# Letting every late place of two step lists take side steps that need exp and log

## The chip, the cores and the metric

The kernel runs on one core of a Trainium2 chip. The metric is the device time of one execution in microseconds (us), the median of several runs; lower is better. TensorE (PE in the profile, with its weight loads as PEld), VectorE (DVE), ScalarE (ACT), GpSimd (POOL) and SyncE (SP) each work through their own list of instructions in order. They wait for each other by semaphores.

## The reference

Two layers of a sequence model, each a mixer and a feed-forward part with a residual around both, on 4 sequences of 256 tokens with 512 features (1024 tokens in all):

1. retention: projections q, k, v, gate; rotary embedding; decay-weighted attention in chunks of 128; RMS norm; output projection.
2. a router: softmax over 64 logits, the 8 largest weights w of each token, `out = flat * w_sum + w_dense @ expert_bias`.
3. a state-space mixer with 128 heads in 8 groups: `proj = x @ in_proj_w.T`, a causal convolution of 4 taps and silu on most of it, per-head steps `dt = softplus(...)`, decays `exp` of cumulated `dt * A`, the chunked product, a gate `silu(gate)`, a group norm and an output projection.
4. low-rank adapters: 64 adapters of rank 16, the 16 best of each token.

In front of each part stands `_layernorm(x)`, and each adds to x. All arithmetic is float32; the large projections are three matmuls each of a high and a low part.

## The kernel before

The tokens are worked on in two halves of 512. Each stage is a pipeline over units that is written out by hand: a list of letters says in which order one turn of the loop emits its pieces of work. A scheduler then orders the instructions of each engine, within what the data and the rotation of buffers in program order allow. Bank "x" of PSUM has two buffers: whatever is allocated there in program order waits until the tile two before it has been read. The same goes for the tags "xn" (one buffer) and "xd" (two).

Stage 3 (the mixer of part 3) has 64 units: a pair of two 128-channel chunks for one half. The order is four pairs of half 0, the same four of half 1, then the halves in turn. A turn `i` works on three pairs: `before` (output projection, O0 to O3, L858), the pair itself (T0, T1: transposes and scaling, L779 to L790; M0, M1: the mixer's matmuls `ps_y`, L804) and `after` (I0, I1: x projections `ps_x`, convolution L714 and L716 and silu; G0, G1: gate projections `ps_g` and silu; X0, X1: sums of the exponents, L294 and L296; D0, D1: their exp, L1122, and the product with C.B, L757; B: `ps_bc`). W casts one weight tile into its high (ACT, L139) and low part (POOL, L142) and starts later loads.

Beside the units runs the **side line**: a queue of generators for work of other parts. In stage 3 its first entries are `route(1)` (the router for half 1: logits L603, softmax L616 to L622, top 8 L627 to L630, transposed weights L634 and L636, update of x L645 to L650) and `prepare3(1)` (half 1 for part 3: load of wdt L690, moments L87 to L92, normalised x L100 to L126, then the softplus steps L217 to L246, and the cumulated sums ps_cum, ps_in, ps_tail L250 to L268). A place P or E in a list calls `pump` (L1133), which runs one step of the queue, up to its next `yield`. A step that has to follow a use of exp or log is announced by `yield True`:

```
def pump(steps=1, table=False):
    while k.side and steps and (table or not k.needs):
        k.needs = next(k.side[0], k)
```

P is `k.pump` and does nothing while the next step needs exp or log; E is `k.pump(1, True)` and takes any step. The reason for two letters is ScalarE's tables: silu sits in one set, exp and log in another, and `act` (L1115 to L1124) puts a table load (L1119) between them and holds all uses of a set together. In a turn the silus come up to G1 and the exps at D0, D1. The side line's PSUM tiles go to bank "x" in stage 3 (`k.bank = BANK3`). Its softmax weights `wT` take a buffer of tag "xd", as `xd` of T0, T1 does; `raw_wdt`, the normalised `xn`, `room` of the softplus and `xe` of T0, T1 all take the one buffer of "xn".

Which list a turn uses is chosen at L926: FILL3 for turn -1, SIDE3 while the queue is not empty, else STEP3. Before the first pair of half 1 is prepared (turn 3), whatever is left in the queue is run off at once (L910, `k.pump(1000, True)`). At the end of the stage the router of part 4 joins the queue, and turns 63 and 64 use SIDE3 again.

Of the kernel before, what the change touches and what calls it, by code (L numbers as in the profile page):

```python
# [18 lines left out]
P = 128  # L19
# [13 lines left out]
STEP1 = "K S0 W T S1 S2 W G0 G1 K C K P U A0 K W P A1 T P P Q0 N0 W W N1 Q1 T T W K D F".split()  # L33
SIDE1 = "S0 W G0 T P K C W W P P W S1 K G1 S2 U P A0 N0 A1 P Q0 T W T F W N1 K Q1 T T D W W".split()
STEP3 = "W T0 T1 B I0 W M0 M1 X0 X1 I1 O0 G0 W W O1 W W P O2 W W G1 P W O3 D0 D1 W W".split()
FILL3 = "B X0 X1 I0 I1 P P G0 G1 W W P P W D0 D1 E E".split()
SIDE3 = "T0 T1 I0 I1 M0 M1 P B X0 X1 P P O0 W O1 G0 G1 W W P O2 O3 W P W P D0 D1 E E".split()

# [615 lines left out]
def state_space(k, tc, io):  # L656
# [239 lines left out]
    def run(done):  # L896


        with tc.tile_pool(name="s3", bufs=1, reuse_waits="tile") as own.only:
            for i in range(-1, len(pairs) + 1):  # L900
# [24 lines left out]
                )  # L925
                for one in FILL3 if i < 0 else SIDE3 if k.side else STEP3:  # L926
                    who = {"T": p, "M": p, "O": before, "P": k, "E": k, "W": k}.get(one[0], after)
# [329 lines left out]
```

## Time and profile before

| | |
|---|---|
| median of 3 runs | 2560.72 us (2560.52 to 2563.05) |
| the profiled execution's own time | 2561.88 us |
| its span, first to last instruction | 2560.1 us |
| mean granted TensorE clock | 0.988 |
| busy: PE, DVE, ACT, POOL | 2459.5, 2070.7, 1534.0, 1539.5 us |
| table loads on ACT | 193, 1283 ns each |
| stage 3 in the span | about 935 to 2440 us |
| its turns with route(1) and prepare3(1) | up to about 1057 us |

Times in the views are microseconds from the span's start. A row of the timeline is: start, duration, engine, line, operation, output<-inputs, shape, and in brackets how long the engine was idle before it and who ended that. A row of waits is: who waited, for whom, sum in us, times, longest. A row of the table by stretches is: stretch, length, then for each engine its busy time and instructions, the granted TensorE clock, the DMA share and rate.

### The profile page before, as it was taken

The numbers are of one execution on the slowest core, as the hardware profiler recorded it, in microseconds if no ns is written. First come the engines' busy times: TensorE is split into PE (matmuls) and PEld (weight loads), VectorE is DVE, ScalarE is ACT, GpSimd is POOL, SyncE is SP. The second block draws the span as 40 slices with busy tenths as digits, with TensorE's granted clock in tenths as the row PEclk, the third lists the DMA queues.
The fourth block names the chain that finished last, engine by engine and source line by source line (L and its number), as shares of the span: only waits on it lengthen the run. The fifth ranks groups of instructions, "written<-read, shape, count | busy, mean of one in ns | idle before, by whom it ended". The sixth has DMA issues, their size and how long they took to land.

```text
span 2560.1 us, 35586 instructions
## 1 busy us (share of the span) xinstructions
PE 2459.5 (96%) x13488; PEld 1991.8 (78%) x13488; DVE 2070.7 (81%) x2694; ACT 1534.0 (60%) x2109; POOL 1539.5 (60%) x996
## 2 busy tenths in 40 slices
PE   7899999999999898899999999999999999999889
PEld 6778787788777686678888888888888888888677
DVE  6787777778788779697988888988988988979963
ACT  3665565566665565475765756666756657657630
POOL 4554444546565547586784865856756756757840
PEclk9999999999999999999999999999999999999989
DMA  3222112212222222242332323222323223313321
GB/s 107 76 71 53 50 50 58 66 58 89 84 92 60 72 91 87 78 124 71 95 91 67 101 73 91 91 72 86 99 66 99 83 67 103 95 61 105 99 70 68
DMA packets 82891, 206.18 MB, mean 81 GB/s; under 512 B 8672, under 2 KB 10592, under 8 KB 82720
## 3 DMA queue, kind: packets, MB, share of 16 engines
q1 hardware_dynamic: 82720, 203.90, 26.6%
q8 instruction: 107, 1.75, 0.3%
q14 instruction: 64, 0.52, 0.1%
HBM read 200.86 MB, written 3.01 MB: 80 GB/s over the span
## 4 chain that ended last, share of the span: by engine, by line
PE 73%; DVE 17%; ACT 3%; POOL 3%; issue 3%; DMA 1%; SPq 0%; POOLq 0%; ACTq 0%; DVEq 0%
PE ps_g L201 16%; PE ps_x L201 11%; PE ps_o L858 10%; PE ps_o L459 6%; PE ps_q L201 6%; PE ps_y L804 5%; PE ps_y L412 3%; PE ps_bc L201 3%; DVE m L757 3%; DVE conv L716 3%; PE ps_sc L400 2%; PE ps_o L1084 2%; PE ps_v L201 2%; PE ps_t L779 2%; DVE m L294 2%
## 5 line engine op out<-in xcount | busy, mean ns | idle before, releaser
L201 PE MATMUL ps_g<-xs_hi,wg_h 128*128 128x512 f32 x768 | 308.8, 402 | 13.7 <-DVE r_q L354 7.3
L201 PE MATMUL ps_g<-xs_lo,wg_h 128*128 128x512 f32 x768 | 304.8, 397 | 0.0
L201 PE MATMUL ps_g<-xs_hi,wg_l 128*128 128x512 f32 x768 | 302.5, 396 | 0.0
L757 DVE TENSOR_TENSOR m<-m,cb 128x1536 f32<-128x1536 f32 x128 | 275.0, 2152 | 30.4 <-ACT m L1122 29.9
L716 DVE SCALAR_TENSOR_TENSOR conv<-ps_x,cw,conv 128x510 f32<-128x510 f32 (+2 forms) x384 | 269.9, 736 | 24.7 <-ACT conv L714 22.2
L1119 ACT ACT_TABLE_LOAD x193 | 247.6, 1283 | 3.9 <-PEq L1245 0.8
L294 POOL TENSOR_TENSOR m<-gb,start 128x512 f32<-128x512 f32 x128 | 152.8, 1196 | 128.5 <-PE ps_y L804 90.2
L142 POOL TENSOR_TENSOR wo_l<-raw_wo,wo_h 128x1024 fp32r<-128x1024 f32 x60 | 152.2, 2537 | 124.1 <-ACT wo_h L139 118.2
L858 PE MATMUL ps_o<-wo_h,yh 128*128 128x512 f32 x512 | 212.8, 416 | 13.0 <-DVE acc L864 11.1
L296 POOL TENSOR_SCALAR_AFFINE_SELECT m<-m 128x1024 f32<-128x1024 f32 x160 | 217.2, 1358 | 1.5 <-DVE m L294 1.4
L832 POOL TENSOR_TENSOR sqs<-sqs,sq 128x512 f32<-128x512 f32 x112 | 186.8, 1668 | 46.5 <-ACT sq L830 46.5
L818 POOL TENSOR_TENSOR xs<-xs,sg 128x512 f32<-128x512 f32 x128 | 204.5, 1597 | 13.8 <-DVE xs L814 13.8
L142 POOL TENSOR_TENSOR wx_l<-raw_wx,wx_h 128x1024 fp32r<-128x1024 f32 x38 | 97.8, 2575 | 178.8 <-ACT wx_h L139 168.5
L201 PE MATMUL ps_x<-xs_lo,wx_h 128*128 128x512 f32 x512 | 205.3, 401 | 0.0
L201 PE MATMUL ps_x<-xs_hi,wx_h 128*128 128x512 f32 x512 | 204.3, 399 | 0.0
L201 PE MATMUL ps_x<-xs_hi,wx_l 128*128 128x512 f32 x512 | 203.9, 398 | 0.0
L858 PE MATMUL ps_o<-wo_l,yh 128*128 128x512 f32 x512 | 203.1, 397 | 0.0
L858 PE MATMUL ps_o<-wo_h,yl 128*128 128x512 f32 x512 | 199.1, 402 | 2.5 <-DVE yl L823 2.5
L142 POOL TENSOR_TENSOR wg_l<-raw_wg,wg_h 128x1024 fp32r<-128x1024 f32 x60 | 152.7, 2545 | 63.9 <-ACT wg_h L139 63.9
L201 PEld LDWEIGHTS ps_g<-xs_hi,wg_h 128*128 128x128 f32 x768 | 144.5, 188 | 56.9 <-issue 17.3
L1122 ACT ACTIVATE xs<-conv,cb 128x512 f32<-128x512 f32 x128 | 90.8, 722 | 162.8 <-DVE conv L716 162.6
L1122 ACT ACTIVATE m<-m 128x1024 f32<-128x1024 f32 (+1 forms) x160 | 181.4, 1134 | 9.7 <-POOL m L296 9.4
(281 smaller groups left out, 6929.3 us busy)
## 6 DMA issues: line engine op xcount, KB each, us to landing
gb<-cum SPq DMA_DIRECT2D x160, 512.0 KB
raw_wx<-in_L_attn_in_x_dram SPq DMA_DIRECT2D x38, 512.0 KB
raw_wg<-in_L_attn_in_gate_dram SPq DMA_DIRECT2D x38, 512.0 KB
raw_wo<-n_L_attn_out_proj_w_dram SPq DMA_DIRECT2D x38, 512.0 KB
raw_wq<-in_L_attn_Wq_dram SPq DMA_DIRECT2D x22, 512.0 KB
raw_wg<-in_L_attn_Wg_dram SPq DMA_DIRECT2D x22, 512.0 KB
raw_wo<-in_L_attn_Wo_dram SPq DMA_DIRECT2D x22, 512.0 KB
raw_wkv<-in_L_kv_dram SPq DMA_DIRECT2D x11, 512.0 KB
```

Of the source, the lines that this page charges most:

```text
L142: nc.gpsimd.tensor_tensor(lo, w, hi.bitcast(F32), ALU.subtract)
L201: tc.nc.tensor.matmul(ps, a[:, c, :], b[:, c, :], start=(c == 0 and n == 0), stop=(c == KC - 1 and n == 2))
L294: engine.tensor_tensor(m[:, blk], gb[:, min(blk, 1)], last(at, P), ALU.add)
L296: nc.gpsimd.affine_select(out=causal, in_=causal, compare_op=ALU.is_ge, fill=GONE, base=0, pattern=[[0, 8], [1, P]], channel_multiplier=-1,)
L459: nc.tensor.matmul(ps, y[:, 2 * h + b, :], w[:, h, :], start=(i == 0), stop=(i == 5))
L716: nc.vector.scalar_tensor_tensor(acc[:, :, j:], ps[:, :, :SEQ - j], cw[:, ch, TAPS - 1 - j:TAPS - j], acc[:, :, j:], ALU.mult, ALU.add,)
L757: made = nc.vector.tensor_tensor(mh, mh, cbs[p.g, p.half].rearrange("p z b l -> p z (b l)").unsqueeze(2) .to_broadcast([P, 3, 2, 2 * P]), ...
L818: nc.gpsimd.tensor_tensor(xs, xs, p.sg[n], ALU.mult)
L832: nc.gpsimd.tensor_tensor(total, total, sq, ALU.add)
L858: nc.tensor.matmul(ps, y[:, at], w[:, n, :], start=(i == 0), stop=(i == 5))
L1119: load = nc.scalar.preload_act_table_set(table)
L1122: ins = nc.scalar.activation(out, in_, func, bias=bias, scale=scale)
```

## The change

In FILL3 the third pair of P becomes E, and in SIDE3 the three P behind G0 and G1 become E. Nothing else is touched.

```
-FILL3 = "B X0 X1 I0 I1 P P G0 G1 W W P P W D0 D1 E E".split()
-SIDE3 = "T0 T1 I0 I1 M0 M1 P B X0 X1 P P O0 W O1 G0 G1 W W P O2 O3 W P W P D0 D1 E E".split()
+FILL3 = "B X0 X1 I0 I1 P P G0 G1 W W E E W D0 D1 E E".split()
+SIDE3 = "T0 T1 I0 I1 M0 M1 P B X0 X1 P P O0 W O1 G0 G1 W W E O2 O3 W E W E D0 D1 E E".split()
```

Counted through the generators, the queue's steps fall on the turns of stage 3 as follows:

| turn | before | changed |
|---|---|---|
| -1 | moments and logits of the router | the same |
| 0 | max and exp; sum and top 8 | the same two, then wT, update of x tiles 4, 5 |
| 1 | wT, x tiles 4 to 7, load of wdt, moments, first normalised tile | x tiles 6, 7, load of wdt, moments, all four normalised tiles |
| 2 | normalised tiles 5 to 7, dt projection, softplus up to log | dt projection, softplus, ps_cum, ps_in, ps_tail |
| 3, run off at once | ps_cum, ps_in, ps_tail | nothing |
| 63, 64 | router of part 4 | the same steps at the same places |

## The prediction

> **What bounds the kernel now.** I read the busy times and the chain first, then the table by stretches, the waits and the timeline around the only place the step table of the change touches, turns 0 to 3 of stage 3.
>
> ```profile
> PE 2459.5 (96%) x13488; PEld 1991.8 (78%) x13488; DVE 2070.7 (81%) x2694; ACT 1534.0 (60%) x2109; POOL 1539.5 (60%) x996
> ...
> PE 73%; DVE 17%; ACT 3%; POOL 3%; issue 3%; DMA 1%; SPq 0%; POOLq 0%; ACTq 0%; DVEq 0%
> ```
>
> TensorE bounds the whole. Turns 0 to 3 are among the few places where it doesn't. The table by stretches (stretch, length, busy PE, PEld, DVE, ACT, POOL, clock, DMA share, GB/s):
>
> ```profile
> 963.80:980.00 16.20, 16.20 (x142) 13.99 (x142) 16.20 (x22) 9.54 (x14) 15.21 (x9) 1.00 0.44 135
> 980.00:1004.00 24.00, 20.41 (x76) 13.14 (x75) 22.64 (x39) 17.88 (x26) 17.22 (x21) 0.93 0.28 96
> 1004.00:1011.30 7.30, 4.79 (x14) 3.37 (x14) 7.15 (x12) 0.00 (x0) 2.79 (x4) 0.77 0.22 72
> 1011.30:1030.00 18.70, 15.21 (x104) 11.61 (x103) 15.19 (x23) 10.54 (x16) 12.69 (x12) 0.91 0.09 30
> 1030.00:1045.50 15.50, 13.73 (x58) 10.05 (x58) 12.33 (x14) 5.22 (x8) 7.12 (x4) 1.00 0.11 34
> 1045.50:1052.50 7.00, 0.05 (x2) 0.03 (x1) 6.79 (x6) 1.55 (x2) 3.86 (x2) 0.74 0.47 150
> ```
>
> From 980 to 1052.5, PE is idle for 3.6 + 2.5 + 3.5 + 1.8 + 7.0 = 18.4 us, and DVE is nearly full where PE is emptiest: the side line paces this part. The longest single wait, from the waits view and the timeline:
>
> ```profile
> PE ps_cum L250 <- DVE e L246: 6.9, 1, 6.9
> ...
> POOL rstd L91 <- DVE mv L89: 6.6, 3, 4.0
> ```
> ```profile
> 1043.00 0.69 DVE L237 SCALAR_TENSOR_TENSOR e<-room,e 128x512 f32<-128x512 f32 x1
> 1044.72 2.44 DVE L238 SCALAR_TENSOR_TENSOR start<-room,start 128x512 f32<-128x512 f32 x1 [1.02 <-ACT start L1122]
> 1047.19 2.72 DVE L240 SCALAR_TENSOR_TENSOR dt<-dt,start 128x512 f32<-128x512 f32 x1
> 1049.83 0.68 DVE L241 TENSOR_TENSOR e<-e,room 128x512 f32<-128x512 f32 x1
> ```
>
> The softplus chain runs on DVE alone while PE stands still. L238 and L240 take 2.44 and 2.72 us where L237, of the same shape, takes 0.69: POOL is splitting wo and wx (L142, 2.4 us each) just then. That surplus I call lock time.
>
> **What the change removes, adds and moves.** No instruction is added: the built program has 193 table loads as before, and the same work on each engine. Turn -1 and turns 63, 64 take the same steps; there only neighbours swap at the very end of the program (6 matmuls of 0.23 us, one store behind one load), for which I allow 1 us either way and take 0. All else is order within about 965 to 1057 us. Three edits decide.
>
> (1) In turn 3 nothing is left to run off; ps_cum follows turn 2's work. (2) The four normalised tiles move into turn 1, in front of turn 2's x projections. (3) wT and the first two updates of x move into turn 0, in front of turn 1's. Edits 2 and 3 have a price: bank "x" rotates in program order through two buffers, so `ps_x` of pair 2 must now wait until `x += ps_o_4` is done, and `ps_x` of pair 3 behind the four transposed tiles. wT also takes the "xd" buffer that the xd of pair 1 needs, so pair 1's `ps_y` waits for the last router matmul. The built order shows it: `ps_x` of pair 2 stands behind ps_o_4 and ps_o_5, `ps_y` of pair 1 behind ps_o_7. On POOL the exponents of pair 2 (L294), which were at 978.6, now stand behind the four pairs of rstd instructions (L91, L92), which wait for DVE's moments. Queued behind them: the gating (L818) that ACT's yh and so `ps_o` wait for, and the splits of wdt and wbc.
>
> I lay the rows of the timeline end to end in the new order, between four marks: end of `ps_y` of pair 0 (966.8), of pair 1 (979.55), of pair 2 (1022.0), start of ps_cum (1052.5). Before: 12.7 + 42.5 + 30.5 = 85.7 us.
>
> First stretch. The logits of tile 7 come some 3 us earlier, at about 973. DVE then: L607 0.2, L616 0.4, L617 0.35, L757 1.75, L620 to L622 1.0, L627 and L628 1.3, L630 and L629 0.7 (to about 980); POOL's nine small ones 2.15, some of it behind L630; four L645 2.9 (to 984.4). PE meanwhile has 24 `ps_o` and 24 `ps_g` (5.6 us each at a start-to-start of 0.233), wT comes at 985, ps_o_4 ends at 987, and its add (0.67) frees the bank at 987.7. Then 24 `ps_x` 5.6 (993.3), ACT L714 0.7, three L716 and an L650 (996.9), ps_o_7 1.1, xd 0.68, xe 0.41, 24 `ps_y` 2.6: about 1001.8. That is 35.0 us: **+22.3**.
>
> Second stretch. POOL sets it: rstd out at about 1001.5, then L294 1.2, L818 1.65, L296 1.3, again 1.2 and 1.65, L832 1.3, L296 1.3, wdt 1.3, wbc 2.35 = 13.3 us (1015); the load of wo takes the buffer that wbc frees, 3.6 us from issue to cast (997.81 to 1001.40), and its cast (1.05) stands in front of xs_hi on ACT; then 0.59 + 0.69 + 0.65 for the tile (1021.6), 48 matmuls of `ps_x` and `ps_y` in their new order 8.4: 1030. That is 28.2 us: **-14.3**.
>
> Third stretch. dt 2.8, then DVE in order: L217 0.74, xd 0.68, L823 0.75, L222 0.69, L232 0.69, xd 0.68 with a wait of 0.6, L757 1.75, L823 0.75, L234 0.43, L237 0.69, L757 1.75, L238 2.44, L240 2.72, L241, L242, L246 0.69 each, L244 0.43, and four L864 of 0.67 that now stand between them = 23.3, say 23.5: **-7.0**. The 6.95 us stall thus shrinks rather than goes: the 18 `ps_o` that now fill PE there bring their L864 into the chain.
>
> Sum **+1.0**. The rows I used for the first two stretches are free of lock time. Before has about 10 us of it between 966 and 1040 (each DVE row less the shortest of its form, summed). How much of it the new order puts on the path no row shows: none gives +1.0, all gives +11. I take a quarter, 2.5, since most lock time there fell where DVE then waited anyway. The lower bound also takes L238 and L240 free (-3.8) and half of wo's landing hidden (-1.8): -4.6. So **+3.5 us**.
>
> The clock: matmuls at 1008.28 start 0.43 us apart instead of 0.23 after a gap of no more than 2.51 us.
>
> ```profile
> 1006.88 0.50 PE L858 MATMUL ps_o<-wo_h,yh 128*128 128x512 f32 x1 [2.51 <-DVE acc L864]
> ...
> 1007.91 0.58 PE L858 MATMUL ps_o<-wo_l,yh 128*128 128x512 f32 x1
> 1008.28 0.63 PE L858 MATMUL ps_o<-wo_h,yl 128*128 128x512 f32 x1
> ```
>
> So many short gaps cost clock as one long gap does (0.64 from 1052.5 to 1057), and I take no gain from dividing the stall. The Trainium skill (TensorE: Matmul & The Clock Gate, "What's actually happening") has the clock halve only after an idle window of about 3.4 us; by it the divided stall would keep the full clock in those 4.5 us, and my estimate from that page would be 1.6 us lower.
>
> Against the profiled execution (2561.88 us, of which 2560.1 is span) +3.5 gives 2565.4; the median of the runs shown lies 1.2 lower, so **2564.2**.
>
> **Rivals.**
> *Faster.* The moved steps find cover: PE's waits of 6.95 (ps_cum) and 2.51 (L864) go, and edits 2 and 3 add only what PE lacks in the first stretch. It has there 17.3 us of work (24 `ps_o`, 24 `ps_g`, two ps_o of the router, transposes, logits) for the 20.7 us until the bank is free: 3.4. Sum -9.5 + 3.4 = -6.1: 2554.6. For it: PE is what fills most of the chain. Against it: DVE is busy 94% from 980 to 1004 and cannot take the router's chain sooner for nothing.
>
> *Slower.* The bank makes pair 2's projections late, POOL's row behind the rstds makes everything of pair 2 late, and all the lock time falls on that path, because POOL's and DVE's queues are now both on it: +11, 2571.7. It decides from a quarter of the 10 us upwards: +5.1 is reached at 4.1 us of lock time. For it: L757 was hit for 1.8 and L823 for 1.0 in a stretch where POOL split wbc, and these now stand side by side with the same split. Against it: the third stretch is shorter by rows that already hold their lock time.
>
> *Nothing changes.* The places take the same steps: true of turns -1, 63, 64, false of turns 0 to 3 by the count of steps; so it gets no chance of its own.
>
> **Numbers.** What a measurement of this kernel can tell from no change is about 0.2%, 5.1 us. Forecast case (-2.8 to +5.1): 0.50. Faster: 0.17, of which 0.12 lies beyond 0.2%. Slower: 0.33, all beyond. So faster 0.12, same 0.55, slower 0.33. The range takes in the lower bound of -4.6 and, above, the slow rival: 2555.5 to 2572.
>
> **What would show it.** Right: PE's wait for L246 at ps_cum falls below about 4 us, `ps_x` of pair 2 starts near 988 instead of 967, `ps_y` of pair 1 ends near 1002, L294 of pair 2 on POOL stands behind L92, and ps_cum starts between 1050 and 1058. Wrong: ps_cum before 1048 (then the lock time and POOL's row were overpriced), or after 1060; a difference made anywhere behind 1060, where both programs have the same order until the last 120 us, would mean that my whole frame misses.

## The result, and the profile after

The changed kernel takes **2576.32 us** (median of 4 runs, 2574.43 to 2579.27); the kernel before took 2561.89 us beside it (4 runs, 2560.52 to 2565.36). The ratio is **1.0049, interval 1.0036 to 1.0061**: slower by 14.4 us by the medians and by 12.6 by the ratio, where +3.5 was forecast. The time lies outside the range given. The profiled execution took 2574.43 us, 2572.7 of it span, at a mean clock of 0.987.

The lines of the page that answer to those shown of before (busy time by engine, then the chain):

```profile
PE 2465.6 (96%) x13488; PEld 1994.2 (78%) x13488; DVE 2076.9 (81%) x2694; ACT 1535.5 (60%) x2109; POOL 1542.9 (60%) x996
...
PE 72%; DVE 16%; ACT 4%; POOL 4%; issue 3%; DMA 1%; SPq 0%; POOLq 0%; ACTq 0%; DVEq 0%
```

As many instructions on each engine as before, and PE busy for 6.1 us more with them. The marks of the prediction (ends of `ps_y` of pairs 0, 1, 2, start of ps_cum) now stand at 965.7, 1002.7, 1038.7 and 1068.4. The table by stretches between these marks, first of the changed kernel, then of the kernel before (stretch, length, busy PE, PEld, DVE, ACT, POOL, clock, DMA share, GB/s):

```profile
965.70:1002.70 37.00, 31.68 (x163) 23.86 (x164) 29.83 (x55) 16.86 (x24) 16.01 (x24) 0.91 0.17 57
1002.70:1038.70 36.00, 23.90 (x121) 16.91 (x121) 25.29 (x27) 15.52 (x21) 20.20 (x13) 0.81 0.22 66
1038.70:1068.40 29.70, 20.82 (x73) 14.72 (x73) 27.82 (x27) 12.15 (x16) 23.03 (x11) 0.83 0.22 71
```
```profile
966.80:979.60 12.80, 12.80 (x107) 10.99 (x107) 12.80 (x18) 8.12 (x11) 11.81 (x7) 1.00 0.38 124
979.60:1022.00 42.40, 35.28 (x169) 24.69 (x169) 37.52 (x63) 21.87 (x32) 25.25 (x30) 0.92 0.23 70
1022.00:1052.50 30.50, 19.31 (x82) 13.86 (x81) 26.98 (x30) 13.32 (x18) 18.82 (x10) 0.89 0.20 68
```

The sum went from 85.7 to 102.7 us, **+17.0**. Subtract PE's busy time from the length: PE stood idle for 26.3 us instead of 18.3 (+8.0) and was busy for 76.4 instead of 67.4 (+9.0), with 354 records between the marks in both. The clock column goes with the second part: length times (1 - clock), summed over the stretches, is 6.8 us before and 15.2 after. So in PE's account about half of the loss is waiting, and the other half is the same matmuls at a lower clock. This says where PE's time went, not yet why: the two can trade places, as in h1_hold below, which loses 1.8 us less to the clock than before and waits 1.3 us more, in the same sum.

In the first stretch two rows come some 21 and 25 us later, both behind the router. `ps_x` of pair 2 starts at 988.30, and the second `xd` of pair 1 (L781) stands right behind the last router matmuls (L649). The changed kernel, then before:

```profile
988.30 0.50 PE L201 MATMUL ps_x<-xs_hi,wx_h 128*128 128x512 f32 x1
...
997.16 1.13 PE L649 MATMUL ps_o<-room,wT 64*128 64x512 f32 x2 [1.42 <-DVE x L650]
...
998.32 0.69 DVE L781 TENSOR_TENSOR xd<-ps_t,dt 128x512 f32<-128x512 f32 x1
```
```profile
967.15 0.48 PE L201 MATMUL ps_x<-xs_hi,wx_h 128*128 128x512 f32 x1
...
973.55 0.68 DVE L781 TENSOR_TENSOR xd<-ps_t,dt 128x512 f32<-128x512 f32 x1
```

Behind turn 3 the two programs run alike: pairs 4, 30 and 62 end 15.5, 15.4 and 15.7 us later than before (`ps_cum` starts 15.9 later, and not 17.0, because the first mark is 1.1 earlier). Some 3 us come back behind that, so that the span is 12.6 longer.

PE's timeline of the changed kernel in the second and third stretch (start, duration, what, and in brackets the idle time before it and who ended it), with the longer waits and three rows without one:

```profile
1005.38 0.50 PE L858 MATMUL ps_o<-wo_h,yh 128*128 128x512 f32 x1 [1.13 <-ACT yh L822]
...
1011.15 0.50 PE L858 MATMUL ps_o<-wo_h,yh 128*128 128x512 f32 x1 [3.75 <-ACT yh L822]
...
1019.65 0.66 PE L108 MATMUL ps_xn<-ident,xn 128*128 128x128 f32 x4 [2.10 <-DVE xn L100]
1021.30 0.65 PE L108 MATMUL ps_xn<-ident,xn 128*128 128x128 f32 x4 [1.00 <-DVE xn L100]
1024.63 1.12 PE L108 MATMUL ps_xn<-ident,xn 128*128 128x128 f32 x4 [2.67 <-DVE xn L100]
1026.38 1.11 PE L108 MATMUL ps_xn<-ident,xn 128*128 128x128 f32 x4 [0.64 <-DVE xn L100]
1027.23 0.77 PE L201 MATMUL ps_x<-xs_hi,wx_h 128*128 128x512 f32 x1
1027.80 0.63 PE L201 MATMUL ps_x<-xs_lo,wx_h 128*128 128x512 f32 x1
1028.22 0.63 PE L201 MATMUL ps_x<-xs_hi,wx_l 128*128 128x512 f32 x1
...
1049.57 0.80 PE L201 MATMUL ps_g<-xs_hi,wg_l 128*128 128x512 f32 x1 [2.73 <-POOL wg_l L142]
...
1060.83 0.80 PE L858 MATMUL ps_o<-wo_h,yh 128*128 128x512 f32 x1 [3.53 <-DVE acc L864]
...
1068.38 1.16 PE L250 MATMUL ps_cum<-upper,e 128*128 128x128 f32 x8 [1.84 <-DVE e L246]
```

The four normalised tiles come one by one, PE waits for each of them for 0.6 to 2.7 us, and then the `ps_x` of pair 3 start 0.43 us apart where 0.23 is the pace at full clock: the short waits are paid a second time in the clock. At the end of the third stretch the waits view has

```profile
PE ps_cum L250 <- DVE e L246: 1.8, 1, 1.8
```

where before had 6.9. The stall that the change aims at is gone, and the stretch is only 0.8 us shorter. The softplus rows on DVE, and the rows of POOL beside them:

```profile
1048.33 2.80 DVE L757 TENSOR_TENSOR m<-m,cb 128x1536 f32<-128x1536 f32 x1 [0.44 <-ACT m L1122]
...
1054.09 1.68 DVE L237 SCALAR_TENSOR_TENSOR e<-room,e 128x512 f32<-128x512 f32 x1
...
1057.35 2.82 DVE L238 SCALAR_TENSOR_TENSOR start<-room,start 128x512 f32<-128x512 f32 x1
...
1060.69 2.26 DVE L240 SCALAR_TENSOR_TENSOR dt<-dt,start 128x512 f32<-128x512 f32 x1
```
```profile
1037.45 1.04 POOL L294 TENSOR_TENSOR m<-gb,start 128x512 f32<-128x512 f32 x1 [13.16 <-PE ps_y L804]
1038.45 2.86 POOL L142 TENSOR_TENSOR wx_l<-raw_wx,wx_h 128x1024 fp32r<-128x1024 f32 x1
...
1055.88 3.74 POOL L142 TENSOR_TENSOR wo_l<-raw_wo,wo_h 128x1024 fp32r<-128x1024 f32 x1 [0.67 <-ACT wo_h L139]
1059.59 2.81 POOL L142 TENSOR_TENSOR wx_l<-raw_wx,wx_h 128x1024 fp32r<-128x1024 f32 x1
```

POOL's L294 of pair 3 waits 13.16 us for pair 2's `ps_y`. Of the splits behind it, three (`wg_l` at 1046.70 and the last two rows) run beside the softplus, of which L237, L238 and L240 take 1.7 to 2.8 us. DVE is idle for only 29.70 - 27.82 = 1.88 us of this stretch, so the length of its rows paces it.

### The profile page after: what moved, and what is told of

It is laid out like the page before. It is cut to its first block, busy times and chain, and to the rows that moved or that the text cites. A ratio compares the mean times of both kernels' runs of the same rounds, so it can differ in the third digit from the quotient of the medians.

```text
span 2572.7 us, 35585 instructions
## 1 busy us (share of the span) xinstructions
PE 2465.6 (96%) x13488; PEld 1994.2 (78%) x13488; DVE 2076.9 (81%) x2694; ACT 1535.5 (60%) x2109; POOL 1542.9 (60%) x996
## 3 DMA queue, kind: packets, MB, share of 16 engines
q8 instruction: 107, 1.75, 0.3%
## 4 chain that ended last, share of the span: by engine, by line
PE 72%; DVE 16%; POOL 4%; ACT 4%; issue 3%; DMA 1%; SPq 0%; POOLq 0%; ACTq 0%; DVEq 0%
PE ps_g L201 15%; PE ps_x L201 11%; PE ps_o L858 10%; PE ps_o L459 6%; PE ps_q L201 6%; PE ps_y L804 5%; PE ps_y L412 3%; PE ps_bc L201 3%; PE ps_sc L400 2%; DVE conv L716 2%; DVE m L757 2%; PE ps_v L201 2%; PE ps_o L1084 2%; PE ps_t L779 2%; DVE m L294 1%
## 5 line engine op out<-in xcount | busy, mean ns | idle before, releaser
L201 PE MATMUL ps_g<-xs_hi,wg_h 128*128 128x512 f32 x768 | 308.9, 402 | 15.4 <-DVE r_q L354 7.1
L757 DVE TENSOR_TENSOR m<-m,cb 128x1536 f32<-128x1536 f32 x128 | 277.4, 2171 | 30.9 <-ACT m L1122 30.6
L294 POOL TENSOR_TENSOR m<-gb,start 128x512 f32<-128x512 f32 x128 | 153.7, 1203 | 142.1 <-PE ps_y L804 103.5
L858 PE MATMUL ps_o<-wo_h,yh 128*128 128x512 f32 x512 | 213.9, 418 | 17.1 <-DVE acc L864 12.2
L832 POOL TENSOR_TENSOR sqs<-sqs,sq 128x512 f32<-128x512 f32 x112 | 187.1, 1671 | 45.8 <-ACT sq L830 45.8
L818 POOL TENSOR_TENSOR xs<-xs,sg 128x512 f32<-128x512 f32 x128 | 205.5, 1606 | 12.5 <-DVE xs L814 12.5
```

Source lines behind the costliest of these rows:

```text
L201: tc.nc.tensor.matmul(ps, a[:, c, :], b[:, c, :], start=(c == 0 and n == 0), stop=(c == KC - 1 and n == 2))
L294: engine.tensor_tensor(m[:, blk], gb[:, min(blk, 1)], last(at, P), ALU.add)
L757: made = nc.vector.tensor_tensor(mh, mh, cbs[p.g, p.half].rearrange("p z b l -> p z (b l)").unsqueeze(2) .to_broadcast([P, 3, 2, 2 * P]), ...
L818: nc.gpsimd.tensor_tensor(xs, xs, p.sg[n], ALU.mult)
L832: nc.gpsimd.tensor_tensor(total, total, sq, ALU.add)
L858: nc.tensor.matmul(ps, y[:, at], w[:, n, :], start=(i == 0), stop=(i == 5))
```

## The experiments

Ratios are to the kernel before on the same chip, with the 95% interval. The three stretches are those between the four marks, in one profiled execution of each kernel; "idle" is PE's idle time in them, "clock" the length lost to a granted clock below 1 in them (summed from the profile's clock records, which is why before and after read 6.9 and 15.4 here).

| run | stretches | sum | idle | clock | ratio |
|---|---|---|---|---|---|
| before | 12.8, 42.4, 30.5 | 85.7 | 18.3 | 6.9 | 1 |
| changed | 37.0, 36.0, 29.7 | 102.7 | 26.3 | 15.4 | 1.0049 [1.0036, 1.0061] |
| h1_hold | 12.8, 42.5, 30.4 | 85.7 | 19.6 | 5.1 | 1.0002 [0.9992, 1.0011] |
| d1_one | 38.6, 32.1, 28.9 | 99.6 | 25.6 | 13.9 | 1.0056 [1.0039, 1.0074] |
| d2_two | 37.0, 33.5, 28.6 | 99.1 | 24.3 | 11.9 | 1.0043 [1.0029, 1.0058] |
| x1_wt | 15.4, 47.3, 29.1 | 91.8 | 22.3 | 8.5 | 1.0047 [1.0032, 1.0062] |
| t3_bank_after | 35.1, 32.4, 28.7 | 96.2 | 27.8 | 17.1 | 1.0091 [1.0074, 1.0108] |
| t4_bank_before | 11.9, 44.5, 39.0 | 95.4 | 24.7 | 14.8 | 1.0089 [1.0074, 1.0104] |
| t5_bank_wt | 12.0, 50.9, 28.6 | 91.5 | 21.0 | 13.2 | 1.0066 [1.0051, 1.0081] |
| t7_local | 12.0, 51.0, 28.5 | 91.5 | 20.9 | 13.1 | 1.0028 [1.0016, 1.0041] |
| n1_wdt | 39.7, 29.4, 30.4 | 99.5 | 25.6 | 13.7 | 1.0063 [1.0047, 1.0079] |
| k1_no_split | 39.7, 32.6, 22.3 | 94.6 | 23.9 | 11.1 | 1.0042 [1.0027, 1.0057] |
| k2_before_no_split | 12.7, 37.5, 27.1 | 77.3 | 12.7 | 3.7 | 0.9969 [0.9959, 0.9980] |
| b1_before_wt | 12.8, 40.1, 30.4 | 83.3 | 17.2 | 5.8 | 0.9983 [0.9973, 0.9992] |
| b1_again | 12.8, 38.4, 30.5 | 81.7 | 17.3 | 4.1 | 0.9985 [0.9975, 0.9995] |
| g1_third | 39.7, 28.0, 30.3 | 98.0 | 27.2 | 9.5 | 1.0035 [1.0021, 1.0049] |
| g2_third_wt | 15.4, 41.4, 30.6 | 87.4 | 19.3 | 6.0 | 1.0028 [1.0019, 1.0038] |
| g3_second | 12.7, 49.1, 29.6 | 91.4 | 17.8 | 13.7 | 1.0009 [1.0000, 1.0019] |
| n2_two_xn | 13.9, 49.6, 26.9 | 90.4 | 23.6 | 8.5 | 1.0040 [1.0026, 1.0053] |
| n3_before_two_xn | 12.7, 46.5, 26.1 | 85.3 | 15.6 | 10.0 | 1.0025 [1.0014, 1.0035] |

The sums and the ratios don't agree to the microsecond: in x1_wt, g2_third_wt, n2_two_xn and n3_before_two_xn they are 5 to 7 us apart. What lies behind pair 63 took 120.4 to 128.5 us outside the runs with bank "o" throughout (before: 123.0), with an order of the last instructions that differs a little from build to build; and pairs 5 to 8 took, outside the runs with bank "o", 89.6 to 89.7 us in some executions and 92.1 to 93.5 in others. One kernel was profiled twice (b1_before_wt and b1_again), and its two sums are 1.6 us apart, so smaller differences between sums say nothing. A sum is compared with a sum, and the whole time with the whole time.

### Is it the exponentials' place, or the advance of the queue?

h1_hold takes exp and log at the new places in turn 0 and then no further step, so that the queue is not ahead from turn 1 on. d1_one and d2_two go ahead by one step (wT) and by two.

```
h1  turn 0: ... W W E O2 O3 W E W D0 D1          (two steps, then none)
d1  turn 0: ... W W P O2 O3 W P W E D0 D1 E E    (one E)
d2  turn 0: ... W W P O2 O3 W E W P D0 D1 E E    (one E, a place earlier)
```

> Turn 0 of SIDE3 takes its two steps with exp (max and exp; sum and top 8) at the places behind the gates, as the changed kernel does, and then takes no further step: the queue is where the kernel before has it at the end of turn 0. Theory A (the loss comes from advancing the queue by three steps, whose tiles then stand in front of pair 2's in the rotation of bank x and of tag xd): same as before, 2559 to 2564 us. Rival B (the loss comes from the place of the exp itself, the table load that moves up in front of the silus): 2570 to 2576 us.

> In turn 0 only the last of the three places may take steps with exp: the queue is advanced by one step, wT, instead of three. Theory A: wT then holds the xd buffer that pair 1 needs until the last router matmul, and ps_t of the router stands in bank x in front of ps_x of pair 2, but no update of x does: a large part of the loss, 2566 to 2573 us. Rival C (the loss is lock time between VectorE and GpSimd that happens to fall on the path, with no order in the number of steps): anywhere, not between the kernel before and the changed one in step with the advance.

> In turn 0 the middle one of the three places may take steps with exp: the queue is advanced by two steps, wT and the update of one tile of x. Theory A: between the advance by one and the full change, 2568 to 2576 us. Rival C: no order.

h1_hold has the time and all three stretches of before: the early exp and log cost nothing. d1_one, with wT in turn 0 and each later step one place earlier, has most of the loss in the sum (99.6) and all of it in the whole time (1.0056). In the whole time one step ahead, two or the three of the change make no order that can be told from noise, though more loss had been expected from more steps: what matters is that the queue leaves turn 0 ahead at all.

### The buffers: wT, bank "x", and the load of wdt

x1_wt takes wT of half 1 out of tag "xd"; t3 and t4 move the side line's PSUM tiles to bank "o", in the changed kernel and in the one before; t5 does both in the changed kernel, t7 both, with bank "o" in turns 0 to 3 alone; b1 moves wT in the kernel before; n1 loads wdt into a "y" buffer.

```
x1, t5, t7, b1:  wT  tag="xd"  ->  tag="y" if half else "xd", bufs=4 if half else 2
t3, t4, t5:      BANK1, BANK3 = "o", "x"  ->  "o", "o"
t7:              k.bank = ("o" if i < 4 else BANK3) if i >= 0 else "o"
n1:              raw_wdt  tag="xn", bufs=1  ->  tag="y", bufs=4   (half 1)
```

> The changed kernel, but wT of half 1 takes a buffer of tag y (four buffers) instead of xd (two). Theory A, part xd: ps_y of pair 1 no longer waits for the last router matmul and ends near 980 to 985 instead of 1002.7 in the span; a third to two thirds of the loss goes, 2564 to 2570 us. If bank x alone carries the loss: no gain, 2573 to 2577 us.

> The changed kernel, with the PSUM tiles of the side line moved from bank x to bank o, so that the x projections of pairs 2 and 3 no longer rotate with the router's tiles. Theory A (the loss comes from buffers that rotate in program order: bank x holds back ps_x, wT in xd holds back ps_y of pair 1): ps_x of pair 2 starts near 967 again, but ps_y of pair 1 still ends near 1000 because wT keeps the xd buffer; ps_cum near 1062 to 1068, ratio to the kernel before 1.002 to 1.005. Rival Q (the loss comes from the order of the queues of DVE and POOL, in which the router's and the normalising rows stand in front of the pairs' rows, whatever the buffers are): no gain, ps_cum at 1066 to 1070, ratio 1.004 to 1.006.

> The kernel before, with the same move of the side line's PSUM tiles from bank x to bank o: the control of the bank. Theory A: in the kernel before bank x held nothing back, so the time is within 0.2% of it, ps_y of pair 1 ends near 980 and ps_cum near 1052. Rival: bank o has a price of its own, since ps_o of the pairs then rotates with the router's tiles: ratio 1.002 to 1.005, ps_cum 1055 to 1060.

> The changed kernel with both buffers freed: the side line's PSUM tiles in bank o, and wT of the second half in the y buffers instead of xd. Theory A: the two buffers are the whole loss, so ps_y of pair 1 ends near 982, ps_cum comes at 1050 to 1056 and the ratio is 0.998 to 1.001. Rival Q (the queues' order on DVE and POOL): ps_cum at 1060 or later and a ratio of 1.003 or more. Rival T (the x2 of the tail: what is gained in this stretch is lost in the last pairs, as it was with wT alone): ps_cum at 1050 to 1056, but a ratio of 1.003 or more with the difference made behind 2400.

> The changed kernel with wT in y and the side line's PSUM tiles in bank o, the latter in turns 0 to 3 only; from turn 4 on they are in bank x as before. Theory A (the two buffers are most of the loss): three stretches together near 91.5 us as with bank o throughout, the last part behind pair 63 back at 121 to 125 us instead of 136, ratio 1.001 to 1.003; what is left of the loss is the four normalised tiles in front of pair 2's ps_y. Rival: the late part does not come back, ratio 1.005 or more.

> The kernel before with wT of the second half in a y buffer instead of xd: the control of the run that moved wT in the changed kernel. If y costs nothing by itself: ratio 0.999 to 1.001 and the same stretches as before. If one more tile in y shifts the later pairs and the tail (that run lost 3 us behind ps_cum beside the changed kernel): ratio 1.001 to 1.003, with the loss behind ps_cum.

> The changed kernel with the load of wdt taken from the single xn buffer (which pair 1's xe releases late) into a y buffer, so that it can land early. If the late load of wdt, for which ACT waited 1.75 us in front of a cast and of yh, carries the second stretch, ps_y of pair 2 ends 2 to 5 us earlier than 1038.7, and ps_cum as much earlier than 1068.4 (ratio 1.003 to 1.004). If it is one of several rows that are late together, the stretch keeps its length within 1 us (ratio 1.0045 to 1.0055).

With wT out of "xd" the first stretch falls from 37.0 to 15.4, and with bank "o" alone (t3) it stays at 35.1, though `ps_x` of pair 2 then starts at 970.2: it was wT's buffer that held back `ps_y` of pair 1. But the second stretch grows to 47.3, and 91.8 of the sum remain against 83.3 when before gets the same help (b1): 8.5 us have another cause.

The whole time of x1_wt did not fall at all: 2574.82 us, where 2564 to 2570 was expected, and a ratio of 1.0047 against 1.0049. In its trace pair 0 ends 3.3 us later than in the changed kernel, and the parts from `ps_cum` to pair 63 and behind pair 63 take 3.5 and 3.4 us more; how much of this is scatter, and how much the price of one more tile in "y", isn't shown. So the buffer's effect on the stretches is shown, and an effect on the whole time is not.

My theory that the two buffers are the whole loss was **not borne out**: freeing bank "x" as well (t5) leaves the sum at 91.5. It isn't refuted either, for bank "o" is no clean way to take bank "x" out. It costs before 9.7 us in these stretches, and 135 us instead of 123 behind pair 63; t7 shows the latter by having it back (124.9). With 1.0028, t7 has the lowest whole time of all runs that keep the whole change.

x1_wt and t5 also clear POOL of one charge. With `ps_y` of pair 1 free, L294 of pair 2 starts at 978.13 in t5, ahead of all the rstd rows. So its place behind them in the changed kernel goes with the late `ps_y`, whose buffer of m it needs.

n1_wdt shortens the second stretch by 6.6 us, to 29.4: the late load of wdt (ACT waits 1.75 us for it, in front of a cast and of yh) was on that path. But the first stretch grew by 2.7, the sum fell by 3.2, and the whole time did not fall (1.0063).

### POOL's splits beside DVE

In k1 and k2 the low parts of six weights, numbers 88 to 93, are written by ACT as a scaled copy, so that part of the computation is changed.

```
-    nc.gpsimd.tensor_tensor(lo, w, hi.bitcast(F32), ALU.subtract)
+    nc.scalar.activation(lo, w, AF.Copy, scale=2.0 ** -13) if onact else nc.gpsimd.tensor_tensor(...)
```

> The changed kernel, in which the low parts of six weights (the ones split on POOL between 1002 and 1068: wbc and wx and wg of the next pair, wo of two pairs, one more wx) are not raw minus high: ACT writes a scaled copy of raw in their place, so that part of the computation is changed, and POOL has six splits of 2.3 to 3.7 us less beside DVE. The stretches of the changed kernel are 37.0, 36.0 and 29.7 us. Theory L (what was missed in stretches 2 and 3 is time that DVE's rows take longer beside POOL's splits): stretch 2 loses 3 to 5 us (the L757 of 3.83 and the L100 of 2.58 fall to 1.8 and 0.6), stretch 3 loses 3 to 5, ps_cum near 1060, ratio 1.001 to 1.003. Rival D (waits for data set the stretches: casts, loads and rstds in one row): each stretch changes by less than 1.5 us, ps_cum at 1066 or later, ratio 1.004 or more.

> The kernel before with the same six low parts written by ACT as a scaled copy (the same part of the computation is changed): the control of the run beside it. Its stretches are 12.8, 42.4 and 30.5 us. Theory L: the softplus rows L238 and L240 fall from 2.44 and 2.72 to 0.7, stretch 3 loses 3 to 5 us, the time falls by 3 to 6 us (ratio 0.9975 to 0.999); if it falls as much as the changed kernel does, the rows lengthened by the splits are no part of the loss. Rival D: within 0.1% of the kernel before.

The softplus rows of k1, to be held against 2.82 and 2.26 above:

```profile
1056.51 0.69 DVE L238 SCALAR_TENSOR_TENSOR start<-room,start 128x512 f32<-128x512 f32 x1
...
1057.87 0.69 DVE L240 SCALAR_TENSOR_TENSOR dt<-dt,start 128x512 f32<-128x512 f32 x1
```

So the splits do lengthen the rows, and the third stretch loses 7.4 us without them. But the sum falls by 8.1 in the changed kernel and by 8.4 in the one before: **the splits cost both about the same, and don't make the difference**, which is 17.3 us without them. (In the changed kernel the fall is 10.8 us in the second and third stretch, while the first grew by 2.7.) In the whole time, too, the two kernels come no closer without the splits: 1.0042 against 0.9969. As the cause of the difference my slower rival ended here. Other rows of POOL, such as L818 and L832, ran beside DVE in k1 and k2 as well, and no run takes them away.

### One edit at a time

g1 does edit 3 alone (turn 0 as changed, turn 1 then waits until the queue is at its old place); g3 does edits 1 and 2 alone; g2 is g1 with wT in "y"; n2 is x1_wt with two buffers by turns for the normalised tiles of half 1.

```
g1, g2  turn 1: ... P B X0 X1 P O0 W O1 G0 G1 W W O2 O3 W W P D0 D1 E E   (turn 2 as before)
g3      turn 0 as before; turn 1: ... P B X0 X1 P P P P O0 W O1 G0 G1 W W P O2 O3 P W P W P D0 D1 E E
n2      normalize(k, tc, half, "3")  ->  normalize(k, tc, half, "3", ("xn", "y") if half else ("xn",))
```

> Edit 3 alone: turn 0 as in the changed kernel (wT and two updates of x in turn 0), then turn 1 takes only what brings the queue back to its old place, so that the four normalised tiles stand in turns 1 and 2 as before. Theory W (wT in xd and the projections behind the router make the loss, edit 2 little): three stretches near 97 to 102 us together (before 85.7, changed 102.7), ratio 1.004 to 1.006. Theory N (the four normalised tiles in front of pair 2's ps_y make half of it): near 92 to 96, ratio 1.002 to 1.004.

> Edit 3 alone, with wT of the second half in a y buffer instead of xd. Theory W with the xd buffer as its only seat: as the kernel before with wT in y (83.3 us for the three stretches, ratio 0.998). If the projections of pair 2 behind the router's two updates (bank x) cost something by themselves: 86 to 91 us, ratio 1.000 to 1.003.

> Edits 1 and 2 alone: turn 0 as before, then turn 1 takes three steps more, so that the four normalised tiles stand in front of pair 2's ps_y and of pair 3's projections, and ps_cum follows turn 2. Theory W: edit 2 costs little, and edit 1 gives back a part: three stretches at 82 to 87 us, ratio 0.998 to 1.001. Theory N: the four tiles pass through one xn buffer in a row in front of ps_y, 91 to 95 us, ratio 1.002 to 1.004.

> The changed kernel with wT in y, and the normalised tiles of the second half in two buffers by turns (xn and one of y) instead of one. With wT in y alone the three stretches were 91.8 us (15.4, 47.3, 29.1) and the ratio 1.0047. If the chain of the four tiles through a single buffer (xn, transpose, cast, difference, next xn) is what holds back ps_y of pair 2, stretch 2 falls by 3 to 6 us and the ratio to 1.002 to 1.003. If the tiles wait for the updates of x anyway, stretch 2 changes by less than 1.5 us.

The table by stretches of g1_third, then of g3_second:

```profile
970.00:1009.70 39.70, 32.84 (x164) 24.02 (x164) 29.86 (x55) 16.92 (x24) 15.57 (x24) 0.87 0.16 54
1009.70:1037.70 28.00, 18.51 (x112) 13.63 (x112) 19.88 (x26) 14.02 (x19) 22.69 (x13) 0.94 0.29 87
1037.70:1068.00 30.30, 19.45 (x80) 13.87 (x80) 26.91 (x30) 13.32 (x18) 18.79 (x10) 0.91 0.19 68
```
```profile
969.00:981.70 12.70, 12.70 (x106) 10.90 (x106) 12.70 (x18) 8.16 (x11) 11.72 (x7) 1.00 0.36 125
981.70:1030.80 49.10, 40.28 (x179) 28.50 (x178) 39.29 (x66) 23.18 (x34) 23.06 (x30) 0.83 0.18 60
1030.80:1060.40 29.60, 20.60 (x75) 14.65 (x73) 27.85 (x27) 12.15 (x16) 23.03 (x11) 0.83 0.20 71
```

The loss comes apart. Edit 3 alone makes the sum 12.3 us longer, edits 1 and 2 alone 5.7; together that is 18.0, and the whole change has 17.0. And the two parts are of different kinds. In g1 PE is idle for 8.9 us more and busy for 3.4 more: it waits. In g3 PE is idle for 0.5 us **less** than before, and busy for 6.2 more (73.6 against 67.4): over the three stretches no waiting was added (1.7 us more in the second, 2.2 less in the third), and the same matmuls ran at a clock of 0.83 instead of 0.92 and 0.89. That the clock makes the 5.7 us is read from this one trace; no run holds the clock fixed. In the whole time edit 3 alone has a ratio of 1.0035 and edits 1 and 2 alone 1.0009, which is just at the edge of what can be told from none. So most of the loss, in the sum and in the whole time, comes with edit 3.

Both expectations of g1_third were met in part: theory W's sum, theory N's ratio. With g3_second it was the other way round. g2_third_wt shows where the waiting of edit 3 sits: with wT out of the way its sum is 87.4, 4.1 to 5.7 above the two traces of b1; so some 7 to 8 of its 12.3 us are the xd buffer. (The whole times of g1 and g2, 1.0035 and 1.0028, can't be told apart.) The rest I put down to pair 2's projections behind the router, which no run shows alone. (The whole time of g2 is above what its sum gives; 125.7 us behind pair 63 are a part of that.) n2_two_xn put the whole chain earlier in PE's order without shortening the second stretch (49.6): the last two tiles stand behind updates of x there, at 1008.85 and 1011.65.

### A version that beats both

> The kernel before with wT of the second half in a y buffer instead of xd, a second time and in more rounds. If the gain of the first time holds: ratio 0.9975 to 0.9990. If that was the scatter between chips: 0.9992 to 1.0010.

> The kernel before with wT in y, and the normalised tiles of the second half in two buffers by turns (xn and one of y). If the single xn buffer paces pair 3's projections and the softplus behind them: three stretches below 82 us (83.3 with wT in y alone), ratio 0.996 to 0.998. If the tiles then all move in front of pair 2's ps_y, as the changed kernel does with them: 86 us or more, ratio 1.000 to 1.002.

The kernel before with wT of half 1 in "y" is faster than both kernels in both of its runs: 0.9983 and **0.9985 [0.9975, 0.9995]**, some 4 us. I take it to remove the same conflict where it bites less: the second stretch is 2.3 and 4.0 us shorter than in the kernel before. A second buffer for the normalised tiles (n3) shortened the third stretch to 26.1 and lengthened the second to 46.5, with the four tiles all in front of pair 2's `ps_y`, as the changed kernel has them: 1.0025 against b1's 0.9985.

## Why the prediction was wrong

**The frame held.** What bounds the kernel, the three edits, the place of the difference (all of it between 966 and 1068) and the price of the first stretch were right: 37.0 us against 35.0 predicted. `ps_x` of pair 2 started at 988.3 (988 predicted), `ps_y` of pair 1 ended at 1002.7 (1002), PE's wait at ps_cum fell below 4 us. ps_cum came at 1068.4, past the 1060 that I had named as the mark of a wrong forecast.

**The step that failed is the sum of the second and third stretch, 28.2 and 23.5 us, measured 36.0 and 29.7**, and in it three terms.

1. **The clock, priced at nothing.** The matmuls of the new order were laid 0.233 us apart throughout, and the clock came in only for the 4.5 us behind `ps_cum` ("I take no gain from dividing the stall"). Divided waits can cost more than one long one: the change put four waits of 0.6 to 2.7 us one behind the other in front of pair 3's `ps_x`, the clock was at half from 1022.0 to 1032.3, and in the three stretches it took 15.4 us instead of 6.9. g3_second shows the clock's part most nearly alone: no more waiting than before, 5.7 us more time. How much of the 15.4 us other waits would have filled isn't shown.
2. **Lock time, counted on one side only.** I laid rows free of it end to end, except for L238 and L240, and compared with a before that is 8.4 us longer for its splits (k2). The changed kernel is 8.1 us longer for them (k1), 10.8 in the second and third stretch, where 6.3 had been allowed: 3.8 in L238 and L240, and the quarter, 2.5. The reason given for the quarter, that in before most lock time fell where DVE waited anyway, doesn't hold: without the six splits the second stretch of before is 4.9 us shorter. The third stretch shows the term best: the splits cost 7.4 us there (k1), and the sum has 3.8. (The split of wx beside L240 took 2.79 us, not the 2.4 that the prediction gives for both.)
3. **The load of wdt.** I gave its split 1.3 us and its landing nothing. Its buffer is the single "xn" one, which pair 1's xe releases only after the late router: with another buffer (n1) the second stretch takes 29.4 us, near the 28.2 of the sum, though the first one grew by 2.7 and nothing of it shows in the whole time.

These overlap, and no run takes all three away together, so I don't add them up to the 14.0 us missed in the two stretches.

**POOL's row.** That L294 of pair 2 behind the rstds sets the second stretch was wrong as a cause, though the order was as foreseen: it needs the buffer that pair 1's `ps_y` releases, and goes ahead of the rstds where that is free (t5).

**The gain of edit 1.** I expected the third stretch to shrink by 7.0. It shrank by 0.8, and by 0.9 in g3: the wait of 6.95 at ps_cum became waits of 2.73 (for a split), 3.53 (for an L864) and 1.84, with half-clock matmuls between them, and DVE's rows were longer.

**The rivals.** "Faster" fell: moved work found no cover. "Slower" had sign and size (+11 against +12.6 in the profiled executions), and its cause was half right: the splits did cost the changed kernel more than the sum allowed (8.1 us in k1 against 6.3), but the kernel before bears as much, so they don't set the two apart.

**What stays open:** what makes the 8.5 us by which x1_wt stays above b1, and how much of it is bank "x"; why x1_wt gained 10.9 us in the sum and nothing in the whole time; why t4 (bank "o" in the kernel before) costs 9.7 us in the stretches. The part behind pair 63 wasn't taken apart either; the 3 us that come back there in the changed kernel I can name only as another order of the last matmuls.

## What to carry to other kernels

Before a queue of side work is let ahead, list the buffers that its next steps take, and ask which of the main line's tiles rotates in the same tag or bank: one small tile (wT) in a two-buffer tag held back a whole unit by more than 20 us. Then look at the whole time too: what wT's buffer gave back in one stretch did not reach it (x1_wt). Price short waits of TensorE at their length and once more at the clock that follows them, and do not call a stall removed until the waits that take its place have been counted. When rows laid end to end are compared with a measured time, both must carry the same contention.

## What the runs showed of the hardware

The granted clock has two values in these traces, 1 and 0.5, and it is at 0.5 for stretches of 3.41 us or a multiple of it, on a fixed grid. In the 20 traces 78 such stretches begin between the end of pair 0's `ps_y` and 50 us behind ps_cum; 66 of them follow a grid window in which PE was idle for less than 3.0 of the 3.41 us, and the middle value is 2.1. The windows of the changed kernel around the four tiles, on that grid:

```profile
1015.21:1018.62 3.41, 2.33 (x10) 1.54 (x9) 3.41 (x2) 1.25 (x3) 3.41 (x2) 1.00 0.29 67
1018.62:1022.04 3.42, 1.31 (x8) 0.84 (x8) 3.27 (x6) 1.58 (x3) 0.78 (x2) 1.00 0.21 86
1022.04:1025.45 3.41, 0.82 (x4) 0.71 (x4) 3.13 (x2) 0.54 (x1) 2.25 (x1) 0.50 0.04 14
1025.45:1028.86 3.41, 2.77 (x10) 2.09 (x9) 2.56 (x5) 1.17 (x2) 0.00 (x0) 0.50 0.42 142
1028.86:1032.28 3.42, 3.42 (x9) 2.46 (x8) 0.03 (x1) 0.00 (x0) 0.00 (x0) 0.50 0.02 5
1032.28:1035.69 3.41, 3.41 (x27) 2.68 (x27) 2.24 (x3) 0.69 (x1) 0.00 (x0) 1.00 0.00 0
```

The window at 1015.21, in which PE was idle for 3.41 - 2.33 = 1.08 us, leaves the clock at 1. The one at 1018.62, idle for 2.11 us in pieces, is followed by half clock, and so is the one after it (2.59 us idle). The third window at half clock follows one that was idle for 0.64 us only, itself at half clock: the state before counts too. In it PE is busy from end to end.

Counted over all grid windows of that part of the 20 traces, the idle time of PE within a window nearly decides. Of 694 windows at full clock none of the 484 with less than 0.6 us of it was followed by half clock, all 41 with 2.1 us or more were, and 37 of the 169 between. A window at half clock was followed by another one in 9 of 87 cases with less than 0.6 us idle, and in all 55 with more.

The Trainium skill (TensorE: Matmul & The Clock Gate, "What's actually happening") gives the window as 3413 ns, free-running, and two states; the traces agree on both. By its table the lower state comes after at least one idle window; here a window that was idle for some two thirds was enough, and the measurement decides.

POOL's split and a DVE row beside it lengthen each other more than I had allowed: L238 and L240 take 0.69 us without splits beside them (k1) and 2.82 and 2.26 with them, and the split of 128x1024 takes 2.3 us at best and 3.74 beside the softplus. Yet in the three stretches it costs both orders about the same, 8.1 and 8.4 us.
